# Normalised tokens transposed by DMA in two of three attention and expert stages, with a new order of work

## The chip, the cores and the metric

The kernel runs on one core of one Trainium2 chip. The core has a matrix engine (TensorE, "PE" in the profile), three engines for elementwise work (VectorE "DVE", ScalarE "ACT", GpSimd "POOL"), a queue engine that issues transfers (SyncE "SP") and 16 DMA engines. The metric is the device time of one execution in microseconds. Before the change it is 3634.33 us, the median of three runs (3633.21 to 3636.59).

## What is computed

The input is 64 sequences of 256 tokens with 256 features, and for each sequence a context of 120 tokens. Everything is in 32-bit floats. The reference applies four gated residual stages, each to layer-normalised tokens:

```python
x = x + tanh(g_xattn[0]) * xattn0(layernorm(x), ctx)   # 16 heads of 64
x = x + tanh(g_ffn[0])   * ffn0(layernorm(x))          # 8 experts, softmax gate with a threshold
x = x + tanh(g_xattn[1]) * xattn1(layernorm(x), ctx)   # 16 heads of 16
x = x + tanh(g_ffn[1])   * ffn1(layernorm(x))          # 8 routed experts, top 2

def layernorm(x, eps=1e-5):
    m, v = mean(x, -1), var(x, -1)
    return (x - m) / sqrt(v + eps)
```

The routed experts of the last stage have indices for 512 tokens only, that is for two sequences, and the kernel applies that stage to group 0 alone.

## The kernel before

**Groups and turns.** Two sequences make a group of 512 tokens, so there are 32 groups, each taken in one turn. A turn has three stages: "front" (the first attention, 16 heads of 64), "middle" (the dense experts) and "back" (the second attention, 16 heads of 16). Group 0 is taken third from last and then goes through the "routed" stage as well. The stages of neighbouring turns overlap.

**Layernorm and its transpose.** `layernorm_T` (L545) makes, for each stage, the normalised tokens with features across the partitions, because a product on PE contracts over partitions. DVE computes the statistics of four tiles of 128 tokens (L569, L563), POOL the reciprocal root (L576, L581), and DVE subtracts and multiplies (L610) into a tile `xn`. Then PE transposes eight blocks of 128x128 against an identity matrix into two accumulator tiles `mm` (L625), and ACT copies each of these into `xnT` (L636): `xnT_f` for front and routed, `xnT_m` for middle, a `late` tile for back. The projections to queries, or the gate and the experts, read `xnT`.

**Softmax weights.** Scores go from PE into accumulator tiles `sp`. DVE takes maxima and subtracts (L661, L666), ACT exponentiates (L671), DVE sums and inverts (L676, L680), POOL multiplies (L685) in place in `ex` or `exb`. In both attentions the weights are then transposed by DMA, in `by_dma` (L708). A DMA transposes numbers of 16 bits, so POOL first copies the weights as 16-bit halves, upper and lower halves apart, into a tile `hv` (L715); SP issues a DMA that transposes `hv` into a tile `tu` (L728); ACT copies the halves from `tu` into their places in `aT` or `aTb` (L721), which PE multiplies with the values. There are two `hv` and two `tu` tiles. One turn has 16 such transposes, eight for each attention.

**The order of the work.** Nothing is run in the order in which the code is written. Every piece of work is a step with an engine, a duration, the steps that it follows and the tiles that it opens or uses. `Plan.ordered` lays all steps out ahead of time: each engine takes, among the steps whose inputs and tiles are there, the one with the smallest due time. A step's due time is its place in its stage's stretch of the turn (constants `FRONT`, `MIDDLE`, `BACK`, `ROUTED`, in turns) less a number from the table `EARLY`, one number for each step of a stage. Four constants (`ALONE`, `PAIR`, `BACK`, `OTHER` in `Plan`) shift due times where PE would change between products on the full array and products on part of it (the scores, the weighted values and the gate's logits use part of it). The resulting order is fixed for each engine; the instructions wait for each other by semaphores. Each engine, and SP's queue, works strictly in this order, so an instruction that waits holds up those behind it.

**Tiles.** `ring(name, n, ...)` makes n tiles that steps take in turn. Two `xn` tiles, one `xnT_f`, one `xnT_m`, two `late` tiles (which hold the second attention's normalised tokens, queries and outputs), four `mm` tiles, two `sp` tiles, four `ex` and two `exb` tiles.

Of the kernel before, what the change touches and what calls it, by code (L numbers as in the profile page):

```python
# [12 lines left out]
U16 = mybir.dt.uint16  # L13
# [4 lines left out]
P = 128  # L18
# [18 lines left out]
FRONT, MIDDLE, BACK = (0.0, 1.158), (1.167, 0.888), (1.784, 1.192)  # L37
ROUTED = 4.551
# [3 lines left out]
        -254, -261, -223, -238, -187, -311, -121, -6, 14, -691, -182, -197, -181, -187, -406,  # L42
        -388, -43, -461, -759, -614, -726, -525, -939, -404, -724, -539, 241, -506, 153, -340, 33,
        -324, 84, -316, -548, -97, -271, -211, -285, 312, 486, 152, -331, -1, -78, -293, 60, 370,
        438, -481, 41, 131, -414, -265, -322, -259, -195, 152, 550, 351, -415, -28, 42, -554, 329,
        348, 578, -516, 261, 190, -534, 55, 117, 22, -210, -208, 151, -267, -58, -207, -329, -104,
        -197, -132, -202, 133, 669, 599, -293, -235, 226, -576, 161, 491, 163, -405, -275, -55,
        -69, 224, -61, -10, 27, -225, 281, 244, 13, -227, -277, -128, -112, 101, -256, -439, 68,
        -239, 77, 67, 8, -774, -146, -287, -352, 350, 323, 246, -666, -288, -166, -212, 240, -17,
        -89, -298, -302, 357, -185, -235, -367, -218, -146, -222, -70, -397, -463, 92, -441, -369,  # L50
        -587, -344, 128, 213, 189,
    ],
    "front": [
        218, -171, -188, -511, -128, -70, 102, -89, 25, 44, -70, -155, -229, 186, -224, -506, -48,
        227, -146, -290, -112, -198, 330, 172, -164, 341, -5, -63, 285, 34, 63, -245, 155, 114,
        249, 307, -181, -26, 23, 230, -500, -440, -96, -49, -141, 360, 258, -592, -408, -106, -21,
        -327, 446, 87, -186, 106, 493, 391, -558, -627, 382, -633, 69, 534, 16, -388, -494, -373,
        -159, -169, 963, 84, 713, -712, 830, -151, 121, 564, -337, 827, -154, 131, -125, 100, 65,
        -58, -522, -519, -403, -289, -324, 86, -4, -785, -603, -790, -230, -259, 320, 285, 485,
        -692, 891, -32, 190, 241, -592, 843, 201, -184, -198, -111, 83, -198, 25, -507, 214,  # L60
        -1381, -696, -688, -747, -536, 26, 434, -519, -704, -497, -274, -354, -198, -408, 946,
        -328, 1156, -366, -462, 193, -791, 362, -465, -348, 217, -61, 326, -543, 258, 1036, 57,
        558, -328, 626, 173, -601,
    ],
    "middle": [
        523, 346, 1097, 1476, 1414, 1804, 1639, 2278, 1440, 878, 103, -62, 963, 1315, 739, 1767,
        1294, 367, 1575, 625, 1449, 635, 537, 1293, 1729, 489, 1432, 1341, 1219, 1031, 695, 1055,
        863, 1128, 1235, 1429, 576, 930, 549, 229, 840, 808, -22, 247, 376, -150, 257, 6, -148,
        -114, -30, -316, -139, -419, -347, 1, -424, -291, -128, 53, -72, -370, -277, -214, -228,
        -485, -161, -296, -260, -138, -469, -400, -231, -509, -57, -125, -287, -240, -265, -8,  # L70
        -170, -229, -714, -117,
    ],
    "back": [
        406, 1217, 1312, 281, 973, 812, 997, 1167, 810, 71, -185, -20, -203, -252, -358, -344,
        -247, -340, 432, 284, 309, 215, -178, 1247, -38, 1602, 310, 1661, 253, 1297, -670, -468,
        -16, -745, -769, -743, 358, 57, 297, -434, -867, -253, 389, 514, -125, 457, 876, -177,
        323, 386, -440, 112, 1284, -78, -78, -1396, -605, -334, 265, -149, 437, -614, -702, -6,
        620, 527, 128, 519, 265, -153, 406, 608, -506, -297, 963, -404, 64, 1087, -300, 48, -1289,
        -899, -90, 164, -140, -324, -871, -693, -3, 266, 502, -600, 583, 35, -9, 16, 167, 448,
        288, 572, -148, -50, -855, -666, -231, -154, 215, 364, -65, 109, 1107, -67, 338, -672,  # L80
        1133, 667, 397, 762, 695, 533, 440, 982, -229, -273, 1407, -222,
    ],
    "routed": [
        698, 669, 584, 449, 96, -216, -130, -264, -55, -285, -110, 6, 323, -358, -7, 352, -114,
        392, -51, 30, 47, 300, 354, -515, 460, 375, 542, 75, 93, 493, 685, 167, 523, 133, -255,
        -115, -81, 737, 938, 1032, 759, 914, 403, 226, 854, 434, -138, 278, -695, 418, 90, -579,
        -114, -443, -366, -434, -593, 429, -111, -381, 51, -261, -405, -181, -101, 20, 209, -111,
        738, 60, 953, 39, 739, 437, -180, 9, -666, -75, 1094, -135, 1443, 199, -171, 807, -190,
        69, 744, 330, -75, 126, -46, 707, 29, 984, -36, 537, -316, -614, 299, -200, -198, 1125,
        -543, 1217, 107, -80, 359, -63, -617, 24, -190, -670, -218, -198, 619, -384, 1174, -14,  # L90
        1881, 1059, 338, 1229, 88, 247, 1646, 150, 1211, -297, -167, 1250, -88, -366, 432, 550,
        257, 200, 374, 1066, -530, 1027, -554, 631, -441, -572, 618, -22, -627, 587, -681, 473,
        -852, -677, 177, -642, -900, -576, -946, -1158, -1256, -1276, -19, -941, -627, -981, -408,
        -264, -1202, 43, -1734, -1264, -646, -1525, -617, -1274, -1855, -586, -1502, -1640, -1800,
        -1022, -1382, -1467, -1019, -188, -1191, 189, -1058, 313, -819, -733, 639, -827, -858,
        296, -585, 290, -288, -691, 387, -583, -217, -322, -328, -608, -714, -445, 474, -872, 862,
        -820, -540, -232, -1276, 213, -1089, -892, -50, -709, -168, -1050, -1349, 706, -1089,
        -515, -265, -53, -200, -922, -523, 1014,
# [5 lines left out]
APART = {"0": ("POOL", 1.79), "1": ("POOL", 1.79)}  # L104
JOINED = {"0": ("ACT", 2.5), "1": ("ACT", 2.5)}
BY_DMA_SEEN = 2.0
HALVES, TURNED = 2, 2
# [36 lines left out]
class Plan:  # L144
# [14 lines left out]
    ALONE, PAIR, BACK, OTHER = 0.257, 0.042, 0.181, -0.047  # L159
# [123 lines left out]
def kernel(  # L283
# [50 lines left out]
    xn_ring = ring("xn", 2, P, NT, D)  # L334
# [210 lines left out]
    def layernorm_T(tk, xnT, after=(), plus_one=False):  # L545
# [58 lines left out]
        def base(t):  # L604
# [3 lines left out]
            tk.reader(  # L608
                t, "DVE", 0.404,
                lambda t=t: nc.vector.tensor_scalar(  # L610
                    xn.tile[:, t, :], tk.x.tile[:, t, :], base(t), rstd(t),
                    ALU.subtract, ALU.mult,
                ),
                [s, *after], opens=[xn, xnT] if t == 0 else [], uses=[ln] if t == 0 else [ln, xn],
                port=True,
            )
            for t in range(NT)
        ]
        ready = []
        for k in range(2):  # L620
# [68 lines left out]
    def transposed(ex, picks, aT, after, which):  # L689
# [3 lines left out]
        def transposes():  # L693
# [11 lines left out]
            [s], uses=[tp, aT], kind="C" + which,  # L705
        )

    def by_dma(ex, aT, after, which):  # L708


        hv, tu = Held(halves_ring), Held(turned_ring)
# [951 lines left out]
```

## Time and profile before

| | |
|---|---|
| median of three runs | 3634.33 us |
| profiled execution | 3636.96 us |
| its span on the core | 3635.3 us |
| PE busy | 3564.3 us (98%) |
| DVE busy | 2758.4 us (76%) |
| ACT busy | 2363.3 us (65%) |
| POOL busy | 2220.3 us (61%) |
| 16 DMA engines, main queue | 45.8% of the span |
| token transposes on PE (L625) | 776 instructions |
| DMA transposes | 512, 4.3 us median from issue to landing |

The span is the time in which the core's engines work; the device time adds 1.7 us around it. The engines work beside each other, so their busy times are not added. A line of the timeline has the start, the length to the end of the last instruction of the run of like instructions, the engine and line, the operation, the tiles written and read, the shape, and the number of instructions; in brackets the idle time of the engine just before it and what ended that. Products on PE are pipelined: one starts before the one ahead of it has ended, so the distance between two starts tells what a product costs, and its own length does not. A 32-bit product is two records, a transpose one.

### The profile page before, as it was taken

What the parts mean: (1) busy time and instruction counts of PE and PEld (TensorE: products, weight loads), DVE (VectorE), ACT (ScalarE), POOL (GpSimd) and SP (SyncE); (2) the same over time, 40 slices, a digit from 0 to 9 for tenths busy, and PEclk for the clock granted to TensorE, in tenths of its full rate; (3) what the DMA queues carried; (4) which work ended last, traced back from release to release, by engine and by line L of the source; (5) the groups of instructions that cost most, each with busy time, mean ns of one, the idle gap of its engine ahead of it and who ended that gap; (6) DMA issues with size and microseconds to landing.
All of it is one profiled execution on the core that took longest, in us unless ns stands there. A gap on an engine that the chain in (4) does not pass through costs nothing.

```text
span 3635.3 us, 54065 instructions
## 1 busy us (share of the span) xinstructions
PE 3564.3 (98%) x20813; PEld 2348.5 (65%) x20813; DVE 2758.4 (76%) x4981; ACT 2363.3 (65%) x2325; POOL 2220.3 (61%) x1530
## 2 busy tenths in 40 slices
PE   7999999999999999999999999999999999999997
PEld 5666666666666666666666666666666666666544
DVE  5577777887777787777788777788777788777876
ACT  4566667666667666666667666776666766666633
POOL 4455556665556665556666556666556666555666
PEclk9999999999999999999999999999999999999999
DMA  6334444554444554444454444544444444444533
GB/s 169 59 70 84 88 93 82 96 96 87 92 86 84 93 96 85 91 88 85 96 100 89 85 87 88 98 96 92 87 86 93 84 96 96 85 88 81 116 64 82
DMA packets 1103266, 328.54 MB, mean 90 GB/s; under 512 B 1068544, under 2 KB 1083296, under 8 KB 1103008
## 3 DMA queue, kind: packets, MB, share of 16 engines
q1 hardware_dynamic: 1103008, 325.08, 45.8%
q8 instruction: 164, 2.69, 0.3%
q14 instruction: 94, 0.77, 0.1%
HBM read 39.80 MB, written 16.78 MB: 16 GB/s over the span
## 4 chain that ended last, share of the span: by engine, by line
PE 79%; DVE 6%; DMA 5%; ACT 4%; POOL 4%; issue 2%; SPq 1%; POOLq 0%; DVEq 0%; ACTq 0%
PE mm L543 68%; PE sp L543 9%; DMA tu<-hv 5%; ACT aT L721 3%; POOL hv L715 2%; PE mm L625 2%; DVE sum L661 2%; DVE sum L676 1%; DVE ex L666 1%; SPq L728 1%; POOL exb L685 0%; POOL ex L685 0%; DVE vsp L1227 0%; ACT aTb L721 0%; ACT exb L671 0%
## 5 line engine op out<-in xcount | busy, mean ns | idle before, releaser
L543 PE MATMUL mm<-ew,xnT_m 128*128 128x512 f32 x2048 | 959.1, 600 | 3.6 <-DVE xt L1172 3.3
L685 POOL TENSOR_TENSOR exb<-exb,sum 128x960 f32<-128x960 f32 x256 | 458.6, 1792 | 534.8 <-DVE sum L680 361.7
L721 ACT COPY aTb<-tu 120x2048 uint16<-120x2048 uint16 x256 | 636.2, 2502 | 79.7 <-DMA tu<-hv 79.6
L721 ACT COPY aT<-tu 120x2048 uint16<-120x2048 uint16 x256 | 631.1, 2499 | 68.2 <-DMA tu<-hv 67.1
L661 DVE TENSOR_REDUCE sum<-sp 128x8 f32<-128x960 f32 x512 | 570.8, 1140 | 123.2 <-PE sp L543 120.3
L1172 DVE SCALAR_TENSOR_TENSOR xt<-mm,w_s,xt 128x256 f32<-128x256 f32 x1024 | 486.3, 478 | 226.5 <-PE mm L543 212.8
L543 PEld LDWEIGHTS mm<-ew,xnT_m 128*128 128x128 f32 x2048 | 374.0, 190 | 372.5 <-issue 334.1
L685 POOL TENSOR_TENSOR ex<-ex,sum 128x960 f32<-128x960 f32 x256 | 456.8, 1795 | 217.8 <-DVE sum L680 191.9
L543 PE MATMUL mm<-xnT_f,wq 128*128 128x256 f32 x2048 | 481.9, 381 | 0.0
L715 POOL COPY hv<-ex 128x1920 uint16<-128x1920 uint16 x256 | 454.1, 1788 | 40.6 <-DMA tu<-hv 40.0
L543 PEld LDWEIGHTS mm<-xnT_f,wq 128*128 128x128 f32 x2048 | 385.7, 190 | 125.6 <-issue 81.9
L543 PE MATMUL mm<-wo,ao 128*128 128x256 f32 x2048 | 463.8, 382 | 0.0
L715 POOL COPY hv<-exb 128x1920 uint16<-128x1920 uint16 x256 | 457.1, 1793 | 8.1
L543 PEld LDWEIGHTS mm<-wo,ao 128*128 128x128 f32 x2048 | 384.2, 190 | 83.0 <-issue 34.3
L866 ACT COPY qT<-mm 128x512 f32<-128x512 f32 x256 | 149.1, 582 | 308.2 <-PE mm L543 308.1
L676 DVE TENSOR_REDUCE sum<-exb 128x8 f32<-128x960 f32 x256 | 290.3, 1144 | 38.9 <-ACT exb L671 38.4
L676 DVE TENSOR_REDUCE sum<-ex 128x8 f32<-128x960 f32 x256 | 291.6, 1140 | 18.6 <-ACT ex L671 18.1
L543 PE MATMUL mm<-wv,ct 128*120 128x512 f32 (+1 forms) x768 | 303.6, 532 | 0.0
L666 DVE TENSOR_TENSOR ex<-sp,sum 128x960 f32<-128x960 f32 x256 | 288.7, 1148 | 0.2
L666 DVE TENSOR_TENSOR exb<-sp,sum 128x960 f32<-128x960 f32 x256 | 287.0, 1142 | 0.0
L543 PE MATMUL mm<-ct,wk 128*128 128x240 f32 x1280 | 286.1, 368 | 0.0
L671 ACT ACTIVATE exb<-exb 128x960 f32<-128x960 f32 x256 | 254.6, 1006 | 47.7 <-DVE exb L666 45.7
(115 smaller groups left out, 4504.4 us busy)
## 6 DMA issues: line engine op xcount, KB each, us to landing
xt<-in_x SPq DMA_DIRECT2D x32, 512.0 KB, 4.8
out_x<-xt SPq DMA_DIRECT2D x32, 512.0 KB, 3.1
tu<-hv SPq DMA_TRANSPOSE x512, 4.3
ct<-in_ctxT SPq DMA_DIRECT2D x32, 240.0 KB, 2.7
v<-in_gu_w SPq DMA_DIRECT2D x8, 512.0 KB, 7.9
ew<-in_expert_w SPq DMA_DIRECT2D x2, 1024.0 KB, 8.9
wk<-in_wkT SPq DMA_DIRECT2D x1, 1024.0 KB
wv<-in_wvT SPq DMA_DIRECT2D x1, 1024.0 KB
```

The source lines that it names most:

```text
L543: return [nc.tensor.matmul(**t) for t in terms]
L625: nc.tensor.transpose(tp.tile[:, t * P : (t + 1) * P], xn.tile[:, t, k * P : (k + 1) * P], ident,)
L661: lambda: nc.vector.tensor_reduce(per_head(0), scores(), AX.X, ALU.max),
L666: lambda: nc.vector.tensor_tensor(weights(), scores(), wide(0), ALU.subtract),
L671: lambda: nc.scalar.activation(ex.tile, ex.tile, AF.Exp, scale=scale),
L676: lambda: nc.vector.tensor_reduce(per_head(8), weights(), AX.X, ALU.add),
L685: lambda: nc.gpsimd.tensor_tensor(weights(), weights(), wide(8), ALU.mult),
L715: return copy[APART[which][0]](hv.tile.rearrange("p (h c n) -> p h c n", h=2, c=8)[:, :, :, :NK], ex.tile.bitcast(U16).rearrange("p (c n h ...
L721: return copy[JOINED[which][0]](aT.tile.bitcast(U16).rearrange("p (c n h) -> p h c n", h=2, c=8)[:NK], tu.tile[:NK].rearrange("p (h c) n - ...
L728: "SP", 2.6, lambda: nc.sync.dma_start_transpose(tu.tile, hv.tile),
L866: lambda ps=ps, qT=qT: nc.scalar.copy(qT.tile.rearrange("p c n -> p (c n)"), ps.tile),
L1172: return nc.vector.scalar_tensor_tensor(xs, ps.tile[:, i * D : (i + 1) * D], w.tile[:, t, e : e + 1], xs, ALU.mult, ALU.add,)
```

## The change

`layernorm_T` gets a parameter `which`: "first" (the first turn's front), "F" (front of every other turn), "M" (middle), "B" (back) and "routed". Those in `TURN = "FB"` no longer use PE. Their normalised tokens go through `by_dma`, as the softmax weights do: one POOL copy of all 2048 halves of a partition into `hv`, one DMA transpose into `tu`, one ACT copy into `xnT`. That is 31 layernorms of the front and 32 of the back; the other 34 (the first one, 32 of the middle, the routed one) keep the transposes on PE. So that one copy serves all eight blocks, the normalisation writes `xn` with the two halves of the features apart. `by_dma` takes the number of columns as an argument (120 for weights, 128 for tokens), and for tokens it opens `xnT` already at the POOL copy. On the PE path `xnT` is opened by the first transposes and no longer by the first normalisation.

The order is laid out anew: other stretches for the stages, other tables `EARLY`, other shifts for the changes of PE's shape. So the steps of all engines and of SP's queue stand in another order.

```diff
-FRONT, MIDDLE, BACK = (0.0, 1.158), (1.167, 0.888), (1.784, 1.192)
-ROUTED = 4.551
+FRONT, MIDDLE, BACK = (0.0, 1.148), (1.152, 0.891), (1.859, 1.21)
+ROUTED = 4.624
...
-APART = {"0": ("POOL", 1.79), "1": ("POOL", 1.79)}
-JOINED = {"0": ("ACT", 2.5), "1": ("ACT", 2.5)}
+APART = {"0": ("POOL", 1.79), "1": ("POOL", 1.79), "L": ("POOL", 1.9)}
+JOINED = {"0": ("ACT", 2.5), "1": ("ACT", 2.5), "L": ("ACT", 2.5)}
 BY_DMA_SEEN = 2.0
-HALVES, TURNED = 2, 2
+TURN = "FB"
+HALVES, TURNED, XNS = 2, 2, 2
...
-    ALONE, PAIR, BACK, OTHER = 0.257, 0.042, 0.181, -0.047
+    ALONE, PAIR, BACK, OTHER = 0.267, -0.003, 0.185, -0.1
...
-    xn_ring = ring("xn", 2, P, NT, D)
+    xn_ring = ring("xn", XNS, P, 2 * NT * P)
...
                 lambda t=t: nc.vector.tensor_scalar(
-                    xn.tile[:, t, :], tk.x.tile[:, t, :], base(t), rstd(t),
+                    xn.tile.rearrange("p (k t n) -> p t k n", k=2, t=NT)[:, t],
+                    tk.x.tile[:, t, :].rearrange("p (k n) -> p k n", k=2), base(t), rstd(t),
                     ALU.subtract, ALU.mult,
                 ),
-                [s, *after], opens=[xn, xnT] if t == 0 else [], uses=[ln] if t == 0 else [ln, xn],
+                [s, *after], opens=[xn] if t == 0 else [], uses=[ln] if t == 0 else [ln, xn],
...
+        if which in TURN:
+            return [by_dma(xn, P, xnT, applied, "L", of_halves=[xnT])]
...
-    def by_dma(ex, aT, after, which):
+    def by_dma(ex, n, aT, after, which, of_halves=()):
...
-                hv.tile.rearrange("p (h c n) -> p h c n", h=2, c=8)[:, :, :, :NK],
-                ex.tile.bitcast(U16).rearrange("p (c n h) -> p h c n", h=2, n=NK),
+                hv.tile.rearrange("p (h c n) -> p h c n", h=2, c=8)[:, :, :, :n],
+                ex.tile.bitcast(U16).rearrange("p (c n h) -> p h c n", h=2, n=n),
...
-                aT.tile.bitcast(U16).rearrange("p (c n h) -> p h c n", h=2, c=8)[:NK],
-                tu.tile[:NK].rearrange("p (h c) n -> p h c n", h=2),
+                flat().bitcast(U16).rearrange("p (c n h) -> p h c n", h=2, c=8)[:n],
+                tu.tile[:n].rearrange("p (h c) n -> p h c n", h=2),
...
         s = step(
             "SP", 2.6, lambda: nc.sync.dma_start_transpose(tu.tile, hv.tile),
-            [s], opens=[tu, aT], uses=[hv], kind="D" + which, seen=BY_DMA_SEEN,
+            [s], opens=[tu] if of_halves else [tu, aT], uses=[hv, *of_halves], kind="D" + which,
+            seen=BY_DMA_SEEN,
         )
...
-        xnT_in = layernorm_T(tk, xnT, plus_one=True)
+        xnT_in = layernorm_T(tk, xnT, plus_one=True, which="M")
...
-        xnT_in = layernorm_T(tk, xnT, ahead[-1:])
+        xnT_in = layernorm_T(tk, xnT, ahead[-1:], which="B")
...
-        xnT_in = layernorm_T(tk, xnT, after)
+        xnT_in = layernorm_T(tk, xnT, after, which="routed")
...
-            xnT_in = layernorm_T(tk, xnT)
+            xnT_in = layernorm_T(tk, xnT, which="first")
```

## The prediction

> **What bounds the kernel now.** I read the page first (share of each engine, then the chain that ended last), then three stretches of the run side by side, the groups of instructions by form, PE's own sequence in one repeating turn, and what the DMA queue and ACT did at the one place where PE waits in that turn.
>
> ```profile
> span 3635.3 us, 54065 instructions
> PE 3564.3 (98%) x20813; PEld 2348.5 (65%) x20813; DVE 2758.4 (76%) x4981; ACT 2363.3 (65%) x2325; POOL 2220.3 (61%) x1530
> ...
> PE 79%; DVE 6%; DMA 5%; ACT 4%; POOL 4%; issue 2%; SPq 1%; POOLq 0%; DVEq 0%; ACTq 0%
> ```
>
> PE is busy nearly all the time and is 79% of the chain. The three stretches (start, repeating turns, end; the columns are length and then PE, weight loads, DVE, ACT, POOL) say where it is not:
>
> ```profile
> 0.00:114.00 114.00, 90.81 (x541) 68.27 (x542) 61.82 (x115) 51.10 (x59) 53.59 (x56) 0.96 0.54 145
> 114.00:3408.00 3294.00, 3275.73 (x19419) 2169.67 (x19418) 2539.76 (x4598) 2216.06 (x2181) 2027.60 (x1386) 1.00 0.46 89
> 3408.00:3635.30 227.30, 197.80 (x857) 110.52 (x855) 156.83 (x271) 96.15 (x87) 139.08 (x91) 0.93 0.39 86
> ```
>
> Idle PE time: 114.0 - 90.8 = 23.2 us at the start, 3294.0 - 3275.7 = 18.3 us in some 30 turns (0.6 us a turn), 227.3 - 197.8 = 29.5 us at the end. In the turns, then, time is PE work and little else, and what the change does to PE's work is what it does to the time. Busy sums overlap, so I price PE steps by the distance between first starts:
>
> ```profile
> 2039.93 1.04 PE L625 MATMUL mm<-ident,xn 128*128 128x128 f32 x8
> 2040.89 2.05 PE L543 MATMUL sp<-kT,qT 64*128 64x120 f32 x32
> 2042.87 1.09 PE L625 MATMUL mm<-ident,xn 128*128 128x128 f32 x8
> ...
> 2047.16 1.88 PE L543 MATMUL mm<-ew,xnT_m 128*128 128x512 f32 x4
> 2048.88 0.27 PE L1100 MATMUL mm<-ident,gate 128*128 128x128 f32 x1
> ...
> 2057.59 1.88 PE L543 MATMUL mm<-ew,xnT_m 128*128 128x512 f32 x4
> 2059.40 1.09 PE L543 MATMUL sp<-kbd,late 32*128 32x240 f32 x16
> 2060.42 3.72 PE L543 MATMUL mm<-xnT_f,wq 128*128 128x256 f32 x16
> 2064.41 1.95 PE L543 MATMUL mm<-aT,v 120*64 120x256 f32 x16 [0.27 <-ACT aT L721]
> ```
>
> An expert pair takes 2048.88 - 2047.16 = 1.72 us before another full-array step, but 2059.40 - 2057.59 = 1.81 us before a step on part of the array: leaving the full array costs 0.09. Eight token transposes before such a step take 2040.89 - 2039.93 = 0.96, so 0.96 - 0.09 = 0.87 us, 0.109 each.
>
> The 0.27 us in the last line is the repeating turn's wait. The queue and ACT just before it:
>
> ```profile
> 2053.41 0.38 SPq L407 DMA_DIRECT2D out_x<-xt  x1
> 2053.94 5.03 SPq L728 DMA_TRANSPOSE tu<-hv  x2
> ...
> 2059.21 2.49 ACT L721 COPY aT<-tu 120x2048 uint16<-120x2048 uint16 x1 [0.67 <-DMA tu<-hv]
> 2061.87 2.49 ACT L721 COPY aT<-tu 120x2048 uint16<-120x2048 uint16 x1 [0.17 <-DMA tu<-hv]
> ```
>
> Two transposes are issued right behind the 512 KB store of x, ACT waits for both, and PE for ACT.
>
> **The change, part by part.** Its own time is 3636.96 us for the profiled execution (span 3635.3), 2.6 above the median 3634.33 of the three; I add the changes to 3636.96 and take 2.6 off.
>
> *Removed from PE.* 63 layernorms (31 first-attention ones after the first turn, 32 second-attention ones) lose eight transposes each: 504 x 0.109 = 55.0 us, all on PE's path. The groups
>
> ```profile
> L625 PE MATMUL mm<-ident,xn 128*128 128x128 f32 x776 | 112.3, 281 | 16.4 <-DVE xn L610 16.0 <-DVE xt L761 0.5
> L721 ACT COPY aT<-tu 120x2048 uint16<-120x2048 uint16 x256 | 631.1, 2499 | 68.2 <-DMA tu<-hv 67.1
> L715 POOL COPY hv<-ex 128x1920 uint16<-128x1920 uint16 x256 | 454.1, 1788 | 40.6 <-DMA tu<-hv 40.0
> L1136 DVE SCALAR_TENSOR_TENSOR w_s<-w_s 128x32 f32<-128x32 f32 x32 | 49.6, 1550 | 1.1
> ```
>
> would allow 504/776 x 112.3 = 73 us; that is the other end, and I keep 55.0 since the records overlap. The Trainium skill ("TensorE: Matmul & The Clock Gate", Part 4: PE-mode transpose) gives about 275 ns for one 128x128 transpose in a kernel; by it 139 us would go and the kernel would land near 3496, which the spacing of 109 ns here contradicts. The 126 accumulator tiles that the transposes opened are free for other steps, a gain I set at nothing.
>
> *Moved on PE.* The new order holds 399 excursions from the full array to part of it against 371 now, and 163 direct changes between partial shapes against 189: in a repeating turn 12 and 5 against 11 and 6. One excursion costs 0.09 to leave, as much again in the partial step at each of its ends (a score step is 0.89 between its like, 1.09 alone), and 0.10 on re-entry: 0.39. A direct change saved is 0.17 by the same steps. 28 x 0.39 - 26 x 0.17 = 6.5; summing every step of both orders by its own kind and neighbours gives +7.2, which I take (ends 5 and 9). A repeating turn holds 107.6 us of PE work now and 106.1 after. The trace agrees for now: the block of 120 products in the chain recurs at 2207.89, 2315.68 and 2423.27.
>
> *Added on POOL.* 63 copies that pull the halves apart, 128x2048: 1.788 x 2048/1920 = 1.91 each, 120 us; POOL goes from 2220 to 2340, 65% of the new span. Each waits for four DVE normalisations; behind it stand a softmax multiply or a bias add. Hidden by PE's work unless DVE is held (rival 2).
>
> *ACT.* 126 copies out of PSUM at 0.59 (74 us) go, 63 joins at 2.5 (158 us) come: +83, to 2446, 68%. A join waits at ACT's head for its DMA; behind the second attention's stands the gate's exponential, behind the first's the next softmax exponential. Cover: the order puts 8.3 us of PE work between the first attention's join and its first projection and 7.0 for the second's, against 2.5 needed.
>
> *SP and DMA.* 575 transposes instead of 512, about 18 a turn for 16; q1's share rises from 45.8% to about 51%. The whole new path (1.9 POOL, 4.3 median from issue to landing, 2.5 ACT) is 8.7 us; the order leaves 14.5 and 15.1 us of PE work for it. The tu tiles are held 8.2 us on average from issue to the end of the join, so 18 of them use 147 of two tiles' 212 us. On SP the second attention's new transpose has a ct load right behind it that waits for PE, and behind that two transposes of softmax weights; the first attention's has only transposes behind it. I price both at nothing as long as the leads above hold, and rival 3 is what a late one costs.
>
> *DVE.* The normalisation writes two pieces of 128; 0.409 each as now, at most 0.05 more, under 0.2 us a layernorm, hidden like the rest of DVE (76%).
>
> *Waits in the turns (18.3 now).* Now the tightest transpose has 6.5 us of PE work from its issue to its product and needs 4.3 + 2.5 = 6.8. In the new order the least in a repeating turn is 9.1, and the x store and load follow that pair instead of preceding it. One product is closer at the end: 3.5 us of PE work from a query projection to it, against 0.6 + 2.5 + 0.1 on ACT. I take -7; ends: all gone, -18; every turn like the worst ones now (1.75 us each, 30 turns = 52), +34.
>
> *Start and end.* Start: the first product still waits for the first transpose behind the weight loads (10.1 us now); 0, ends -5 and +4. End: the last group's projection gains filler, 34 us of PE work behind its last expert pair for 17 now, but its path is 8.7 - 1.5 = 7 us longer; 0, ends -12 and +14 (two groups).
>
> Sum: -55.0 + 7.2 - 7 = -54.8; 3636.96 - 54.8 = 3582.2 on the profile, 3580 at the median (-1.5%). The likeliest case's own range is 3562 to 3605.
>
> **The rivals.** *1, the waits return.* Eighteen transposes on the same two hv and two tu tiles meet the x traffic somewhere else in each turn and every turn loses 1.75 us: 3580 + 7 + 34 = 3621, still faster. For it: landings of up to 7.5 us now. Against: the median of 4.3 and the 9.1 us above. 0.11.
>
> *2, POOL holds DVE; slower.* L1136 above writes 32 numbers in 1550 ns, its neighbour L1144 of the same shape in 211: it stood while POOL ran. If each of 63 new copies holds, for half its length or more, a DVE instruction that PE waits for, the loss is 63 x 0.95 = 60, 3640, to 63 x 1.91 = 120, 3700. It decides from 62/63 = 0.98 us a copy upward. Against: DVE has 24% idle and PE's waits name it rarely. 0.06. The Trainium skill ("SBUF — State Buffer", Who interferes with whom) says the shared port pair goes whole to the one that issues first; this trace agrees at L1136, and the rule speaks against adding POOL work.
>
> *3, ACT's queue; slower.* If a join stands late in every turn as the worst landing does (7.0 - 4.3 = 2.7 us), 31 x 2.7 = 84: 3664. It decides at 2.0 us a turn. 0.03.
>
> *4, no change:* waits eat 1.8 us a turn, 0.04. That the change does not do what it says is excluded by the order, in which 504 PE transposes are gone.
>
> **How the numbers follow.** The forecast has 0.76. About 0.2% is what a measurement here can tell from no change. Faster by more: 0.76 + 0.11 = 0.87; within: 0.04; slower: 0.06 + 0.03 = 0.09. Range: 3562 (waits in the turns gone and the end better) to 3621 (rival 1).
>
> **What would show it.** Right: 20309 matmuls; the repeating block 106 to 107 us apart; idle PE in the turns under 20 us; POOL near 2340 and ACT near 2446 busy; joins of xnT_f and late without PE behind them. Wrong: PE's idle time above 100 us; a wait of PE on the new joins or on DVE's normalisation in each turn; DVE's small operations longer than now; transposes landing well above 4.3 us.

## The result, and the profile after

The changed kernel takes 3603.35 us (median of four runs, 3603.21 to 3604.39) against 3635.46 us for the kernel before (four runs, 3633.21 to 3637.23): a ratio of 0.9912, 95% interval 0.9896 to 0.9927, or 32 us less. The forecast was 3580 us with a range of 3562 to 3621: the direction is right, and 23 us of the forecast gain did not come. The profiled execution takes 3604.39 us, its span is 3602.7 us. The page after, with busy times and the shares of the chain:

```profile
span 3602.7 us, 53270 instructions
...
PE 3524.1 (98%) x20309; PEld 2291.3 (64%) x20309; DVE 2774.2 (77%) x4981; ACT 2428.9 (67%) x2262; POOL 2334.4 (65%) x1593
...
PE 82%; DVE 6%; DMA 4%; POOL 3%; ACT 3%; issue 2%; POOLq 0%; SPq 0%; DVEq 0%; ACTq 0%
```

The 504 matmul records are gone, and POOL and ACT stand within 6 and 17 us of the forecast. The same three stretches as before (start, turns, end; columns as in the prediction):

```profile
0.00:114.00 114.00, 93.88 (x537) 68.52 (x538) 70.51 (x123) 53.02 (x60) 55.76 (x57) 0.94 0.56 149
114.00:3376.00 3262.00, 3246.00 (x18979) 2121.07 (x18979) 2556.19 (x4607) 2283.68 (x2123) 2142.49 (x1447) 1.00 0.53 100
3376.00:3602.70 226.70, 184.22 (x795) 101.75 (x793) 147.53 (x253) 92.24 (x81) 136.20 (x91) 0.91 0.38 86
```

PE's idle time is 20.1 us at the start (23.2 before), 16.0 in the turns (18.3) and 42.5 at the end (29.5). So the end is where time was lost: 13 us more idle time there than before. The groups that the change touches, and who PE waits for:

```profile
L629 PE MATMUL mm<-ident,xn 128*128 128x128 f32 x272 | 37.9, 282 | 22.4 <-DVE xn L611 22.3
L723 POOL COPY hv<-xn 128x2048 uint16<-128x2048 uint16 x63 | 119.3, 1894 | 47.4 <-DVE xn L611 46.7 <-DMA tu<-hv 0.7
L732 ACT COPY late<-tu 128x2048 uint16<-128x2048 uint16 x32 | 80.0, 2499 | 0.2 <-DMA tu<-hv 0.2
L732 ACT COPY xnT_f<-tu 128x2048 uint16<-128x2048 uint16 x31 | 78.5, 2532 | 50.2 <-DMA tu<-hv 50.2
L1150 DVE SCALAR_TENSOR_TENSOR w_s<-w_s 128x32 f32<-128x32 f32 x32 | 7.7, 240 | 1.1
L1147 DVE TENSOR_TENSOR w_s<-w_s,gate 128x32 f32<-128x32 f32 x32 | 29.5, 921 | 0.1
```

```profile
PE mm L544 <- ACT aT L732: 24.4, 22, 8.4
PE mm L629 <- DVE xn L611: 22.3, 3, 11.1
PE mm L544 <- POOL qT L1533: 17.5, 4, 9.5
PE mm L544 <- ACT aTb L732: 7.2, 3, 6.4
```

The columns of the second fence are the total wait, the times and the longest, all in us but the count. The first two rows of the kernel before, for comparison:

```profile
PE mm L543 <- ACT aT L721: 23.8, 17, 10.1
PE mm L625 <- DVE xn L610: 16.0, 6, 11.1
```

No row of the changed kernel names the new joins (xnT_f, late): PE does not wait for the tokens that come by DMA. It waits for the softmax weights of the first attention (aT), and a few times long.

**One table for all kernels.** The prediction priced every PE step of an order by its kind, its size and its neighbours, with the median distances between first starts in the trace of before. I use the same prices for each kernel's own order, so that two things come apart: the PE work that an order holds, and what the distances between steps exceed their price by (every excess over 0.08 us counted). Start is the first 114 us, end the last 240 us up to the last PE step. The excess holds waits and, at the start and the end, a slower granted clock (0.91 at the end after the change, 0.93 before).

| kernel | time, us | PE work priced | excess: start | turns | end |
|---|---|---|---|---|---|
| before | 3635.5 | 3538.8 | 16.5 | 20.8 | 40.8 |
| changed | 3603.4 | 3490.9 | 16.0 | 24.6 | 53.3 |
| end_fit | 3591.5 | 3491.2 | 16.4 | 24.1 | 40.6 |
| pe_again | 3652.2 | 3546.7 | 14.2 | 13.6 | 51.4 |
| pool_twice | 3616.9 | 3490.9 | 16.6 | 35.2 | 55.0 |
| act_twice | 3628.2 | 3490.9 | 17.5 | 47.9 | 55.4 |
| dma_twice | 3734.1 | 3490.9 | 21.3 | 150.1 | 55.8 |
| dma_twice_late | 3672.5 | 3490.9 | 19.7 | 86.9 | 53.2 |
| join_late | 3605.2 | 3490.9 | 16.2 | 26.0 | 52.6 |
| shifted | 3601.6 | 3497.9 | 15.4 | 17.3 | 52.7 |
| before_replanned | 3609.0 | 3540.2 | 10.1 | 6.9 | 32.9 |
| only_first | 3620.3 | 3539.8 | 15.4 | 10.6 | 35.1 |
| only_second | 3597.9 | 3504.9 | 11.4 | 13.7 | 50.3 |
| replanned | 3573.0 | 3485.8 | 12.1 | 22.1 | 33.0 |

PE work gave 47.8 us, and 15.9 came back as excess: 12.5 at the end, 3.8 in the turns, 0.4 less at the start. That leaves the 32. (2.4 of the 3.8 is 29 times 0.08 us at one pair of steps, just over the limit of what is counted.)

### The profile page after: what moved, and what is told of

The parts are those of the page before. It is cut to its first block, busy times and chain, and to the rows that moved or that the text cites. A ratio compares the mean times of both kernels' runs of the same rounds, so it can differ in the third digit from the quotient of the medians.

```text
span 3602.7 us, 53270 instructions
## 1 busy us (share of the span) xinstructions
PE 3524.1 (98%) x20309; PEld 2291.3 (64%) x20309; DVE 2774.2 (77%) x4981; ACT 2428.9 (67%) x2262; POOL 2334.4 (65%) x1593
## 3 DMA queue, kind: packets, MB, share of 16 engines
q1 hardware_dynamic: 1234048, 358.12, 51.9%
## 4 chain that ended last, share of the span: by engine, by line
PE 82%; DVE 6%; DMA 4%; POOL 3%; ACT 3%; issue 2%; POOLq 0%; SPq 0%; DVEq 0%; ACTq 0%
PE mm L544 72%; PE sp L544 9%; DMA tu<-hv 4%; ACT aT L732 2%; DVE sum L683 2%; POOL hv L723 1%; DVE sum L668 1%; POOL ex L692 1%; DVE ex L673 1%; PE mm L629 1%; DVE exb L673 0%; DVE xt L1186 0%; ACT ex L678 0%; POOL exb L692 0%; ACT late L1280 0%
## 5 line engine op out<-in xcount | busy, mean ns | idle before, releaser
L723 POOL COPY hv<-ex 128x1920 uint16<-128x1920 uint16 x256 | 453.1, 1784 | 17.2 <-DMA tu<-hv 11.5
L544 PE MATMUL mm<-wv,ct 128*120 128x512 f32 (+1 forms) x768 | 292.8, 524 | 0.5 <-ACT late L1372 0.5
L544 PEld LDWEIGHTS mm<-ct,wk 128*128 128x128 f32 x1280 | 242.7, 192 | 70.9 <-issue 56.0
```

The lines of the kernel that those rows point to most:

```text
L544: return [nc.tensor.matmul(**t) for t in terms]
L723: return copy[APART[which][0]](hv.tile.rearrange("p (h c n) -> p h c n", h=2, c=8)[:, :, :, :n], ex.tile.bitcast(U16).rearrange("p (c n h) ...
```

## The experiments

### The end: order or path?

The longest gap of the changed kernel is 11 us near span 3391, ahead of the last group's middle-stage transposes, which are still on PE. POOL there:

```profile
3392.90 3.51 POOL L723 COPY hv<-exb 128x1920 uint16<-128x1920 uint16 x2
3396.38 0.23 POOL L577 TENSOR_SCALAR ln<-ln 128x4 f32<-128x4 f32 x1
3396.57 2.34 POOL L782 TENSOR_TENSOR xt<-xt,bo 128x1024 f32<-128x1024 f32 x1
3398.86 1.04 POOL L582 TENSOR_TENSOR ln<-ln,mhalf 128x4 f32<-128x4 f32 x1
```

The reciprocal root that PE's next work needs waits behind two copies of softmax weights and a bias add, some 5 of the 11 us. That is an order, not a length of a path; so the theories were that the tables are bad at the end (A) or that the longer path has no cover there (B).

`end_fit` gives the last two turns and the routed stage numbers of their own, found by a random search on the order that the kernel's own rules lay out:

```diff
-        plan.end_stage(turn + BACK[0], BACK[1], EARLY["back"])
+        plan.end_stage(turn + BACK[0], BACK[1], EARLY.get(f"back{turn}", EARLY["back"]))
```

(the same for "middle"; another `ROUTED`; new numbers under "routed", "middle30", "middle31", "back30", "back31").

> The changed kernel with other numbers in the planner's tables for the last two groups' middle and back stages and for the routed stage alone; no instruction is added or removed, and the first thirty turns keep their order. Theory A, that the end got longer because the numbers planned anew fit the end badly (chiefly the POOL queue, where a bias add stands between two steps of the last layernorm): the kernel's own plan falls from 3570.6 to 3557.2, so about 3590 us (3586 to 3596), with the idle time of PE from span 3376 on falling from 42.5 us to about 30. Theory B, that the end is longer because the path over POOL, the DMA queue and ACT has no other work beside it there: no order gets it back, 3600 to 3607 us, and the idle time stays near 42.

Measured: 3591.49 us (ratio to before 0.9877, 0.9863 to 0.9892), 11.9 us less than the changed kernel. The end, cut at the same place as in the changed kernel:

```profile
3376.00:3589.80 213.80, 180.53 (x773) 99.52 (x771) 145.71 (x255) 89.93 (x80) 135.21 (x90) 0.95 0.40 88
```

The span ends at 3589.8, so the idle time is 213.8 - 180.5 = 33.3 us for 42.5, and in the table the end's excess is 40.6, that of before. The 11.2 us gap ahead of the transposes is 1.1 us there; the waits of PE at this place, changed kernel and `end_fit`:

```profile
3402.58 2.42 PE L629 MATMUL mm<-ident,xn 128*128 128x128 f32 x8 [11.04 <-DVE xn L611]
...
3391.96 0.33 PE L674 MATMUL mm<-ident,xn 128*128 128x128 f32 x1 [1.02 <-DVE xn L656]
```

Theory A: no instruction differs, and the end's loss is gone. The prediction's end term was a statement about the path; the order decided. The numbers moved the steps of all engines there, so how much of it is POOL's queue alone is not shown.

### The price of a transpose on PE

`pe_again` puts the transposes back as PE work and nothing else:

```diff
+    def turned_again(xnT, ps):
+        return [
+            nc.tensor.transpose(
+                ps.tile[:, t * P : (t + 1) * P], xnT.tile[:, k, t * P : (t + 1) * P], ident
+            )
+            for k, t in product(range(2), range(NT))
+        ]
...
-                return products(
+                return ([] if m else turned_again(xnT, ps)) + products(
```

> The changed kernel, in its own order, with the eight PE transposes of the normalised tokens put back as pure PE work: ahead of the first query projection of each attention PE transposes the tokens that the DMA brought once more, into the PSUM tile that the projection then overwrites (64 x 8 = 512 transposes; no new wait, nothing read from them). By the price of the prediction, 0.109 us each with the rest of the step unmoved: +55.8 us against the changed kernel, 3659 us; as some of the turns' waits lie right behind, it may be a little less, 3645 to 3660. By the 275 ns each of the Trainium skill's page TensorE: Matmul & The Clock Gate (Part 4): +141 us, 3744 us. If PE had been waiting for other engines anyway: under +30 us.

Measured: 3652.20 us, 48.9 more than the changed kernel. PE's own sequence:

```profile
1904.38 1.04 PE L856 MATMUL mm<-ident,xnT_f 128*128 128x128 f32 x8
1905.26 1.89 PE L544 MATMUL mm<-xnT_f,wq 128*128 128x256 f32 x8
...
1950.56 1.04 PE L856 MATMUL mm<-ident,late 128*128 128x128 f32 x8
1951.43 3.60 PE L544 MATMUL mm<-late,wq 128*128 128x512 f32 x8
```

Eight take 0.88 and 0.87 us from first start to first start, 0.109 each as priced. PE's busy time rises from 3524.1 to 3578.7, 54.6 us for 512; some 11 us of the turns' excess go at the same time (24.6 to 13.6), which is why the whole is 49 and not 56. The 275 ns of the Trainium skill's page (TensorE: Matmul & The Clock Gate, Part 4) would be right for the length of one record, which is 273 to 282 ns here; as the price of a transpose among others it is 2.5 times too high.

### POOL and ACT: work doubled

Both keep the changed kernel's order and issue one new kind of instruction twice.

```diff
-            *APART[which], apart, after, opens=[hv, *of_halves], uses=[ex], kind="P" + which
+            *APART[which], apart_twice, after, opens=[hv, *of_halves], uses=[ex], kind="P" + which
```

> The changed kernel, in its own order, with the POOL copy that splits the normalised tokens of the first and second attention issued twice (63 more copies of 1.894 us, +119 us of POOL work; the result is the same). Theory A, the prediction's: those copies have cover, and what they hold of DVE is not on the path; their joins end 7 to 8 us of PE work ahead of their first reader: 0 to +15 us against the changed kernel, about 3610. Rival, that POOL holds the port or the queue that the path runs through: at least half of the added work comes out, +60 to +119 us, 3663 to 3722.

Measured: 3616.85 us (3615.10 to 3621.82), 13.5 more for 120.6 us more POOL work.

```profile
PE 3527.0 (98%) x20309; PEld 2289.7 (63%) x20309; DVE 2777.1 (77%) x4981; ACT 2429.0 (67%) x2262; POOL 2455.0 (68%) x1656
```

DVE's busy time grows by 2.9 us. One part in nine comes out: the copies have cover, and rival 2 falls.

```diff
-        return step(*JOINED[which], joined, [s], uses=[tu, aT], kind="J" + which)
+        return step(*JOINED[which], joined_twice, [s], uses=[tu, aT], kind="J" + which)
```

> The changed kernel, in its own order, with the ACT copy that joins the halves of the normalised tokens again issued twice (63 more copies of 2.5 us, +158 us of ACT work; the result is the same). Theory A: the join is done 7 to 8 us of PE work ahead of its reader and 2.5 us more fit in; of the aT and aTb joins behind it in ACT's order some have only 2 to 3 us of lead, so a few waits appear: +5 to +20 us against the changed kernel, about 3615. Rival, that ACT's queue is where the path runs: +80 to +158 us, 3683 to 3761.

Measured: 3628.22 us, 24.9 more for 153 us more ACT work, a little over theory A's 5 to 20 and far below the rival. Of the 23 us that the turns' excess grew by, 18.4 stand at one place in 28 turns: in the second attention's output projection, between its two halves, just ahead of the next group's first query projection. The next experiment shows what stands there.

### The DMA transposes doubled, and one ACT copy moved

```diff
+        def turned():
+            made = [nc.sync.dma_start_transpose(tu.tile, hv.tile) for _ in range(2 if which == "L" else 1)]
+            return made
...
-            "SP", 2.6, lambda: nc.sync.dma_start_transpose(tu.tile, hv.tile),
+            "SP", 2.6, turned,
```

> The changed kernel, in its own order, with the DMA transpose of the normalised tokens issued twice in a row, the same bytes to the same place (63 more transposes that land 4.3 us after issue when alone). Theory A: from the DMA's issue to the first reader lie 13 to 14 us of PE work and 6.8 us of them are needed, so the layernorm's own path keeps some 2 to 3 us; what is left is the queue, in which the halves of the attention weights behind it come later: +5 to +25 us against the changed kernel, about 3618. Rival, that the DMA path of these tokens is what PE waits for in the turns: most of 63 x 4.3 us comes out, +150 to +270 us.

Measured: 3734.10 us (3729.58 to 3739.42), 130.8 more: neither theory. The first row of PE's waits, and ACT in one turn:

```profile
PE mm L544 <- ACT late L1376: 76.2, 31, 3.9
```

```profile
1618.59 2.47 ACT L732 COPY xnT_f<-tu 128x2048 uint16<-128x2048 uint16 x1 [6.32 <-DMA tu<-hv]
1620.94 0.36 ACT L1376 COPY late<-mm 128x256 f32<-128x256 f32 x1
```

PE waits for a copy of 0.36 us (`late`, the second attention's output; L1372 in the changed kernel) which does not need the tokens at all. It stands in ACT's order right behind the join of the next group's tokens, and the join holds ACT for 6.3 us until its DMA has landed. In the table's terms 29 gaps of 3.2 us, 93 of the 150 us. Part of the rest is the clock: behind most of these gaps the trace grants PE half its clock for 3.4 us or a little more, so the products there take longer too. The stretch behind the gap shown above:

```profile
1621.30:1624.70 3.40, 3.35 (x8) 2.73 (x9) 1.74 (x3) 1.86 (x3) 0.93 (x1) 0.50 0.79 149
```

The column 0.50 is the granted clock. There are 19 such stretches in the turns, 78 us in all, each behind a gap of 1.7 to 3.9 us, and none in the turns of the changed kernel, whose waits there are 1.5 us at the longest. So the 130.8 us hold some 39 us of lost clock (half of 78, a part of it inside the gaps) and are not all wait. My theory A counted the lead of the join's own reader (13 to 14 us) and left out what is queued behind the join. The Trainium skill says it plainly (PSUM — Partial Sum Buffer, Engine vs sequencer instructions): the queues of ScalarE, VectorE and GpSimd are strictly first in, first out; these 29 gaps agree.

`dma_twice_late` moves that one copy ahead of the join where they are neighbours:

```diff
-    for s in plan.ordered():
+    planned = plan.ordered()
+    for s in [s for s in planned if s.kind == "JL"]:
+        i = planned.index(s)
+        j = next((j for j in range(i + 1, len(planned)) if planned[j].engine == "ACT"), None)
+        if j and planned[j].kind == "AO" and not any(h in planned[i:j] for h in s.heirs):
+            planned.insert(j, planned.pop(i))
+    for s in planned:
```

> The kernel whose DMA transposes of the tokens are issued twice (3734 us), with one thing moved: where the ACT copy of the second attention's output (the copy into late, 0.36 us) stands right behind the join of the next group's tokens in ACT's order, it is put ahead of it; PE's, DVE's and POOL's orders are the same. Theory A, that PE waited for that copy, which stood behind a join that waited for its DMA (29 gaps of 3.2 us, 93 us, before the second half of the output projection): most of the 93 us go, 3640 to 3670 us. Theory B, that PE needs the joined tokens themselves as early as that, or the DMA queue is what is late: the wait only moves to the query projection, 3715 to 3740 us.

Measured: 3672.48 us, 61.6 less, just outside theory A's 3640 to 3670. ACT now, and the first row of PE's waits:

```profile
1590.37 0.37 ACT L1376 COPY late<-mm 128x256 f32<-128x256 f32 x1 [4.16 <-PE mm L544]
1592.62 2.49 ACT L732 COPY xnT_f<-tu 128x2048 uint16<-128x2048 uint16 x1 [1.88 <-DMA tu<-hv]
```

```profile
PE mm L544 <- ACT xnT_f L732: 33.0, 29, 3.4
```

Two thirds of the gaps went with the move (93 to 35 us); what is left is the true wait for the tokens, 1.1 us a turn. A doubled transpose lands 8.7 us after the first issue where a single one takes 4.3, so the doubling adds 4.4. So the path of the first attention's tokens has about 4.4 - 1.1 = 3 us to spare by itself, and less than that for the copy behind it: 4.4 - 3.2 = 1.2 us, or more, as the 3.2 hold some of the slow clock. `act_twice` gives 2.5 - 18.4/28 = 1.8 for the same place.

`join_late` is the same move without the doubled transposes.

> The changed kernel (transposes issued once) with the same move in ACT's order alone, the copy into late ahead of the join of the next group's tokens. In the changed kernel ACT stands idle 1.6 us at each of these joins but PE waits for the copy behind it only 0.5 us in the whole span: -2 to +2 us against the changed kernel, 3601 to 3605 us. If the join's head wait had cost PE there already: -10 us or more.

Measured: 3605.20 us, 1.9 more: nothing gained. In the changed kernel the head of ACT's queue costs PE nothing yet (0.5 us in the whole span); the doubling has shown how near it is.

### What the order is worth without the change, and the parts of the change

All the tables of four kernels were searched on, each against the order that its own rules lay out. `before_replanned` has no transpose moved, `only_first` and `only_second` move one attention's tokens (`TURN = "F"`, `TURN = "B"`), `replanned` moves both and, alone of the four, has its own numbers for the last turns as in `end_fit`. The edits beside the numbers in `EARLY`, in this order:

```diff
-ROUTED = 4.551
+ROUTED = 2.008894
...
-TURN = "FB"
+TURN = "B"
...
-TURN = "FB"
+TURN = "F"
...
-ROUTED = 4.624
+ROUTED = 1.905571
```

> The kernel before, no transpose moved, with the numbers of its tables searched further against its own plan, which then ends at 3595.8 us against 3606.6: the part of a new order alone. Theory A, that order and transposes are separate gains and the plan carries over: 28.9 us above its plan, as the kernel before is, so about 3625 us (3621 to 3629). Theory B, that the kernel before is at the floor of its PE work and only fewer matmuls make it faster: 3632 to 3640 us.

(The kernel before, run beside these four, took 3636.70 us; their differences to it are counted from that.) Measured: 3608.97 us (ratio 0.9925, 0.9908 to 0.9941), 27.7 less than the kernel before, more than either theory had. An order alone, with all 776 transposes on PE, brings nearly as much as the whole change:

```profile
PE 3561.9 (99%) x20813; PEld 2346.2 (65%) x20813; DVE 2863.2 (79%) x4981; ACT 2359.5 (65%) x2325; POOL 2220.8 (62%) x1530
```

PE's priced work is 1.5 us larger, the excess 28 us smaller, half of that in the turns (20.8 to 6.9). Its tightest transpose of softmax weights in a repeating turn has 8.2 us of PE work from issue to product, for 6.5 in the kernel before, where 6.8 are needed. DVE is busy 105 us longer with the same instructions (the normalisations take 539 ns for 409, an operation on four columns 1336 for 170), and the kernel is faster all the same.

> The changed kernel with the second attention's tokens alone by DMA (256 PE transposes fewer than before, not 504), its tables searched against its own plan, which ends at 3574.9 us. By the prediction's term, 256 x 0.109 = 27.9 us of PE work against the kernel before, the time is 3607; by plan and the 29 to 33 us that the chip lies above it, 3604 to 3608. Rival, that a part alone brings less since the waits grow (as a turn whose other layernorm holds PE): 3615 or more.

Measured: 3597.92 us (3594.87 to 3600.73), 38.8 less than before and 5 less than the changed kernel with both parts; the PE work falls by 33.9 us, 27.9 of it the transposes. That is 6 us below the theory's 3604 to 3608, and the rival did not come.

> The changed kernel with the first attention's tokens alone by DMA (248 PE transposes fewer than before), its tables searched against its own plan, which ends at 3595.9 us and would not go lower. By the prediction's term, 248 x 0.109 = 27.0 us, the time would be 3608 us. By the plan, which finds waits in the place of that work where the search of the kernel before reaches the same 3595.8 us: 3625 to 3630, with more idle time of PE between span 114 and 3376 than the 18.3 us of the kernel before. The first says that each transposed tile is worth its PE time wherever it stands, the second that the first attention's part pays only together with the second's.

Measured: 3620.27 us, 16.4 less than before: neither. It is nearer to the second (3625 to 3630) than to 3608, but not for its reason: the turns' excess is 10.6 us, half of that before, and PE's idle time between 114 us and the last 227 us is 3278.0 - 3269.7 = 8.3 us. What is in the place of the 27.0 us is PE work. The order that the search found has 24 more excursions to partial shapes and 88 more direct changes than the kernel before, by the prediction's prices 24 x 0.39 + 88 x 0.17 = 24 us. Whether the first attention's part could pay alone under a better order stays open.

> The changed kernel with all the numbers of the planner's tables searched further against the kernel's own plan, with tables of their own for the last two turns; the steps are the same. The plan ends at 3544.6 us against 3570.6. The theory that the plan's end carries over to the chip (end_fit: 13.4 us less planned, 11.9 us less measured; time less plan 32.8 us for the changed kernel, 34.3 for end_fit): 3577 to 3584 us. Rival, that the plan is now finer than the landings of the DMA transposes allow (4.2 to 6.9 us, planned at 4.6) and the waits return in the turns: 3590 us or more.

Measured: 3573.03 us (ratio to before 0.9826, 0.9811 to 0.9841), 30 us less than the changed kernel: the fastest version here, 4 us below the theory's range. The waits that the rival foretold are there (22.1 us in the turns, for 6.9 in `before_replanned`), but they leave the time far from 3590.

```profile
PE 3506.1 (98%) x20309; PEld 2287.4 (64%) x20309; DVE 2705.8 (76%) x4981; ACT 2420.0 (68%) x2262; POOL 2334.3 (65%) x1593
```

With both orders searched on, the DMA path is worth 3608.97 - 3573.03 = 35.9 us: 54.4 us of PE work less, 17.2 of excess more, 15.2 of it in the turns. About a third of the PE work saved is paid back in waits. How hard each order was searched is not equal, and only `replanned` has numbers of its own for the last turns (its end's excess, 33.0, is that of `before_replanned`, 32.9, all the same); so these differences between orders are good to some us, not to tenths.

### Why the turns still wait

The turns' waits come in runs of neighbouring turns. Of the 21 waits for transposed softmax weights in the turns, 20 stand behind a transpose that took 5.1 to 6.9 us and met an instruction fetch. Joining each DMA transpose's issue and landing with the packets of the queues that fetch instructions (one of them moves 160 blocks of 16 KB, one in 127 matmuls on average) gives, for the turns:

```profile
q1 hardware_dynamic: 1234048, 358.12, 51.9%
q8 instruction: 160, 2.62, 0.3%
q14 instruction: 96, 0.79, 0.1%
```

| transposes in flight beside | before: count, mean us, over 5.2 us | changed: count, mean us, over 5.2 us |
|---|---|---|
| nothing | 286, 4.31, 0 | 327, 4.36, 0 |
| another transfer | 43, 4.81, 13 | 17, 4.71, 0 |
| an instruction fetch | 132, 4.84, 33 | 171, 4.94, 53 |
| both | 14, 5.68, 7 | 28, 5.78, 25 |

In the changed kernel no transpose without a fetch beside it takes over 5.04 us; with one it takes up to 6.6, and beside both up to 6.9. A longer flight also meets a fetch more easily, so the counts alone do not tell cause from effect. `shifted` tests this. Ahead of everything else on PE it runs 64 transposes that nobody reads, so that the blocks of instructions end half a block elsewhere in every turn:

```diff
+    idle = mm_ring.free[0]
+    for _ in range(64):
+        nc.tensor.transpose(idle[:, :P], ident, ident)
```

> The changed kernel, in its own order, with 64 idle transposes of the identity matrix ahead of everything on PE, in the time in which PE waits for its first tokens (nothing reads them). Only one thing changes for the turns: the stream of PE instructions is 64 matmuls longer, and its blocks of 16 KB, which the trace shows fetched every 127 matmuls, end half a block elsewhere in each turn. In the changed kernel the in-turn waits ahead of the first attention's weighted values stand in runs of consecutive turns, at 549 to 893, 1832 to 2176 and 3221 to 3349 us, 12 turns apart. Theory A, that a DMA transpose lands late where it meets an instruction fetch, and that the fetch drifts through the turn: the runs move by six turns, to about 1190 to 1535 and 2475 to 2820 us, and the old places are free of such waits; time 3600 to 3608 us. Theory B, that those waits come from the order of the work or from the data: they stay where they are.

(The times in it count from the start of the record; those of the span are 11 us smaller.) Measured: 3601.55 us. PE's waits between span 540 and 920 and between 1820 and 2200, changed kernel; each line is one stretch:

```profile
PE mm L544 <- ACT aT L732: 6.4, 8, 1.5
...
PE mm L544 <- ACT aT L732: 5.9, 7, 1.5
```

Between 1180 and 1560 and between 2460 and 2840 the changed kernel has no wait at all. In `shifted` the first two stretches have no wait for aT (0.2 us for aTb in each), and the other two have:

```profile
PE mm L544 <- ACT aT L732: 5.6, 8, 1.7
...
PE mm L544 <- ACT aT L732: 4.4, 6, 1.4
```

The runs moved by six turns, as theory A said, with the order of every engine unchanged. And again no transpose without a fetch beside it takes over 5.06 us. The fetch's part in these waits is shown by a shift that was foretold; what in the DMA engines makes a transpose wait for it is not.

## Why the prediction was right or wrong

*PE's work (-55.0 + 7.2 = -47.8): right, to a tenth.* The changed order priced step by step holds 3490.9 us against 3538.8, and the trace keeps to these prices outside of the gaps (0.07 us are left over). `pe_again` confirms the 0.109 us by an intervention. A turn recurs at 106.9 us (the joins of xnT_f at 2300.2 and 2727.8, four turns apart), for 106 to 107 forecast.

*Waits in the turns (-7): wrong.* The excess grew by 3.8, the idle time fell by 2.3; 5 to 11 us missing, by the measure. The step that failed is "in the new order the least in a repeating turn is 9.1" set against a need of 4.3 + 2.5 = 6.8, on both sides. The need: 4.3 is the landing of a transpose that flies alone, one that meets an instruction fetch lands after up to 6.6 us, and with the join that is 9.1. The lead: the pair that was the tightest before has 8.9 us in the trace, about as foretold, but the pair after it has less. From the issue of that pair's second transpose to the moment at which PE is ready for it lie 7.8 us in the median turn, and at the longest waits 7.4 to 7.8. One of these, with the transpose issued at 874.91:

```profile
881.43 2.49 ACT L732 COPY aT<-tu 120x2048 uint16<-120x2048 uint16 x1 [1.34 <-DMA tu<-hv]
883.98 1.08 PE L544 MATMUL mm<-aT,v 120*64 120x256 f32 x8 [1.51 <-ACT aT L732]
```

It lands 6.5 us after its issue and is joined 2.5 us later, 9.0 in all; PE was ready after 7.6. The second pair has 9.3 us of the turns' waits. The first pair has 5.6: there ACT has both joins and another operation of 0.7 us to do between the first landing and PE's product. The forecast's remark that the x traffic moves away from that pair came true (13 late landings beside another transfer alone before, none after), and it was the smaller part of the matter.

*End (0, ends -12 and +14): the term that was mis-sized.* It measured +12.5, near its upper end, and it is not the longer path that I set there but the order, at the longest gap POOL's in the last group's layernorm: `end_fit` gets 11.9 us back with the same instructions, and with both kernels searched the end's excess is the same (32.9 and 33.0). I had looked at what stood behind PE's last expert pair and not at POOL's queue in front of the last reciprocal root.

*Start (0): right,* -0.4. *POOL, ACT, SP and DMA at nothing: right in the changed kernel.* PE waits for no new join; q1's share is 51.9% for 51. The doubled copies cost 13.5 and 24.9 us for 121 and 153 us of work. But "a late one" (rival 3) is nearer than the leads of 8.3 and 7.0 said: from the join's start to its own reader the trace has 6.2 and 7.3 us in the median turn, and the lead that counts is that of the ACT copy behind the first attention's join, 1 to 2 us.

*Rival 2, POOL holds DVE.* The hold is in the trace and moved with the order: the operation at 1550 ns takes 240 now, its neighbour went from 616 to 921, the normalisations from 409 to 528 on average, more than the 0.05 allowed, and are back at 416 in `replanned`, so it is not the split write. The normalisations before and after the change:

```profile
L610 DVE TENSOR_SCALAR xn<-xt,ln 128x256 f32<-128x256 f32 x388 | 149.6, 409 | 138.5 <-POOL ln L597 85.8 <-POOL ln L581 52.7
L611 DVE TENSOR_SCALAR xn<-xt,ln 128x256 f32<-128x256 f32 x388 | 188.5, 528 | 22.9 <-POOL ln L582 12.7 <-POOL ln L598 9.8
```

PE's waits name no step that it stretched in the turns. The Trainium skill's rule (SBUF — State Buffer, Who interferes with whom) agrees with these holds, but what they cost is only read from the slack behind them: `before_replanned` stretches DVE by 105 us and is 27.7 us faster. *Rival 1* did not come: the turns' waits are 0.8 us a turn (24.6 over some 30), not 1.75.

*What the sum could not see.* It took the order before as a given, and that order held 28 us of waits that other numbers in the same tables remove. The change's 32 us are one order and one set of transposes against another; with both orders searched the transposes are worth 36.

## What to carry to other kernels

Where a planner's tables set the order, price an edit between two orders that were both searched, and search the start, the steady turns and the end apart: here the order alone moved the time by 28 us, the end's numbers by 12. A lead is enough only against the slow case of a transfer, not its median, and for whatever stands behind the waiting instruction in its engine's queue, not only for its own reader. To see what slack a new instruction has, issue it twice in the same order: the doubled POOL copy, ACT copy and DMA came out at 11%, 16% and about half of their added time (the DMA's share with the lost clock in it).

## What the runs showed of the hardware

A DMA transpose of 512 KB (128 x 2048 x 2 bytes) in the changed kernel lands after 4.2 to 5.0 us when nothing is beside it and after up to 6.6 us when it meets a fetch of instructions (6.9 with another transfer as well), although the two queues that fetch move 3.4 MB in all and their packets take 0.4% of the 16 engines' time. The fetches follow the count of PE instructions (one in 127 matmul records on average here), so they drift through a loop of work whose count is no multiple of that, and the waits that they cause come in runs of turns, here 12 and 13 turns apart; 64 more matmuls at the start moved them by six turns. So the number of instructions that lie ahead of a loop can move its waits: `shifted` does 9 us of idle work at the start, its turns' excess is 17.3 us for 24.6, and it is no slower than the changed kernel (3601.55 us). A wait can also cost more than itself: behind 19 gaps of PE of 1.7 to 3.9 us in the turns of `dma_twice` the trace grants PE half its clock, mostly for 3.4 us (others of that length have none), while the turns of the changed kernel, with waits of up to 1.5 us, keep the full clock.
